# Transposing the normalised input of a fused attention and FFN block by VectorE and DMAs instead of TensorE

## The chip, the cores and the metric

The kernel runs on one core of one Trainium2 chip. The metric is the device time of one execution, in microseconds (us). Engines are named as the profile does: PE is TensorE, DVE is VectorE, ACT is ScalarE, POOL is GpSimd, SP is SyncE, which here does nothing but issue DMAs (its queue appears as SPq).

## The reference

```
x: (16, 512, 256) f32;  8 heads of 128;  FFN 512 -> 1024 -> 1024 -> 256 with weights +1 / -1
xn = (x - mean(x)) / sqrt(var(x) + 1e-5)                 # over the last axis
q, k, v = xn @ wq, xn @ wk, xn @ wv                      # per head
q, k = rope(q), rope(k)
p = softmax(q @ k.T / 128 with a causal mask);  attn = (p @ v) @ wo
h = s0 * [xn, -xn] @ K0;  h = 2 relu(h)                  # K = where(k, 1, -1)
h = s1 * h @ K1;          h = 2 relu(h)
ffn = s2 * h @ K2
out = x + attn + ffn
```

## The kernel before

Work is cut by batch (16 batches of T = 512 tokens) and head (8). One head of one batch is a *slot*; there are 128, and a head's work is spread over three of them. In slot g TensorE, in this order, projects q and k of head g+1 (`project_qk`), forms the four rows of scores of head g (`score_row`), with pieces of the FFN between the rows, adds head g-2's output projection into y (`project_o`), finishes an FFN tile, and multiplies the probabilities of head g-1 with v (`attend(g-1)`). Heads 0 and 1 of a batch have slots of their own form (`slot_of_head_0`, `slot_of_head_1`), because the FFN of the batch before ends there and y is stored.

The order on TensorE is the order of the program, written out by hand. In the first stretch (the start of batch 0) VectorE's order is written out too; on the other engines and queues a scheduler puts each instruction where its inputs are ready by its own model, earlier program text first. `behind(instruction, after)` only ties an instruction's place to one that must be issued before it; in a slot `reduced` is the last row's maximum and `raised` its exponential.

The probabilities must be transposed before `attend`. `turn(g)` (L308) does that without TensorE: VectorE transposes blocks of 32x32 (L314) into a tile z, and 16 DMAs on SP's queue (L321) carry the blocks from each of four groups of 32 partitions to each other group, into pT. z and pT have two buffers each. SP's queue also carries the load of x (L88) and the stores of out (L375).

The normalised input of the next batch is transposed by TensorE: `layernorm` runs in slot 4 of a batch, and in slot 6 `transpose_xn` (L218) makes 8 transposes of 128x128 against an identity (L229) into PSUM. VectorE copies them to xnT (L230), and ScalarE and VectorE split xnT, scaled, into a high and a low half xh, xl (L236, L237), which the first FFN layer `ffn0` (L391) streams in two passes. `project_qk`, in slot 7 for the next batch, and `project_v` read xnT. x of the next batch is loaded in slot 1, into one of two buffers, and the other still holds x for the sum with y.

In x's tile token c*128 + p of the batch lies in partition p, column block c.

Of the kernel before, what the change touches and what calls it, by code (L numbers as in the profile page):

```python
# [9 lines left out]
F32 = mybir.dt.float32  # L10
# [12 lines left out]
def kernel(  # L23
# [60 lines left out]
    ps_y = ctx.enter_context(tc.tile_pool(name="ps_y", bufs=1, space=bass.MemoryType.PSUM))  # L84

    def load_x(b):
        t = xpool.tile([P, NT, M], F32, tag="x", name=f"x_{b}")
        nc.sync.dma_start(t, x[b].rearrange("(c p) m -> p c m", p=P))  # L88
        return t


    xs = {0: xpool.tile([P, NT, M], F32, tag="x", name="x_0")}
    for c in range(NT):
        (nc.scalar if c % 2 else nc.sync).dma_start(xs[0][:, c, :], x[0, ts(c, P), :])
    wv_sb = wpool.tile([P, NM, HD], F32, tag="wv", name="wv_sb")
# [3 lines left out]
    def load_w(engine, sb, w, h0, h1):  # L99
# [8 lines left out]

    k0_sb = [
        hpool.tile([P, 2, F0], U8, tag="h1h", name=f"k0_{c}", bufs=2) for c in range(NM)  # L110
    ]
    k1_sb = work.tile([P, NF0, F1], U8, tag="v", name="k1_sb")
    k2_sb = hpool.tile([P, NF1, M], U8, tag="h1l", name="k2_sb", bufs=2)
    wo_sb = wpool.tile([P, H, M], F32, tag="wo", name="wo_sb")
# [8 lines left out]
    for c in range(NM):  # L123
        nc.sync.dma_start(k0_sb[c], k0.rearrange("(i c p) f -> c p i f", p=P, c=NM)[c])
    load_w(nc.sync, wq_sb, wq, 2, H)
# [35 lines left out]
    def make_w0():  # L161
        for c in range(NM):
            kb = hpool.tile([P, F0], F32, tag="h0h", name=f"kb_{c}")
            nc.vector.tensor_scalar(kb, k0_sb[c][:, 1, :], sg_sb[:, 0:1], None, ALU.mult)
            nc.vector.scalar_tensor_tensor(  # L165
                w0_sb[:, c, :], k0_sb[c][:, 0, :], sg_sb[:, 0:1], kb, ALU.mult, ALU.subtract
            )
# [28 lines left out]

    def layernorm(b, after=None):

        xt = xs[b]
        st = small.tile([P, NT, nc.vector.BN_STATS_DIM], F32, tag="st", name=f"st_{b}", bufs=2)  # L200
        mv = small.tile([P, NT, nc.vector.BN_AGGR_DIM], F32, tag="mv", name=f"mv_{b}", bufs=2)
        for c in range(NT):
            begun = nc.vector.bn_stats(st[:, c, :], xt[:, c, :])
            behind(begun, after)
            nc.vector.bn_aggr(mv[:, c, :], st[:, c, :])
        rs = small.tile([P, NT], F32, tag="rs", name=f"rs_{b}", bufs=2)
        nc.gpsimd.tensor_scalar(rs, mv[:, :, 1], LN_EPS, None, ALU.add)
        raised = nc.gpsimd.tensor_tensor(rs, rs, half_sb, ALU.pow)
        xn = npool.tile([P, NT, M], F32, tag="xn", name=f"xn_{b}")
        for c in range(NT):  # L210
            nc.vector.tensor_scalar(
                xn[:, c, :], xt[:, c, :], mv[:, c, 0:1], rs[:, c : c + 1],
                ALU.subtract, ALU.mult,
            )
        xns[b] = xn
        return raised

    def transpose_xn(b):  # L218
        xn = xns.pop(b)
        xnT = npool.tile([P, NM, T], F32, tag="xnT", name=f"xnT_{b}")  # L220
        xh = npool.tile([P, NM, T], F32R, tag="xh", name=f"xh_{b}")
        xl = npool.tile([P, NM, T], F32R, tag="xl", name=f"xl_{b}")
        xnTs[b], halves[b] = xnT, (xh, xl)
        ready = []
        for m in range(NM):
            pool, tag = (ps_t, "t") if b else (ps_s, "s")
            pt = pool.tile([P, T], F32, tag=tag, name=f"pxn_{b}_{m}")
            for c in range(NT):
                nc.tensor.transpose(pt[:, ts(c, P)], xn[:, c, ts(m, P)], ident)  # L229
            nc.vector.tensor_copy(xnT[:, m, :], pt)  # L230
            if b == 0 and m == NM - 1:
                make_scales()
            ready.append(pt)
            if b or m:
                for n, pt in enumerate(ready, m + 1 - len(ready)):
                    nc.scalar.activation(xh[:, n, :], pt, AF.Identity, scale=c_sb)  # L236
                    nc.vector.scalar_tensor_tensor(  # L237
                        xl[:, n, :], xnT[:, n, :], c_sb, xh[:, n, :].bitcast(F32),
                        ALU.mult, ALU.subtract,
                    )  # L240
                ready.clear()
            yield

    Q = 32
    NQ = P // Q
    NB = NT * (NT + 1) // 2  # L250
    vts, qks, probs, pTs, oTs = {}, {}, {}, {}, {}
# [4 lines left out]
    def project_v(b, g):  # L256
        xnT = xnTs[b]
        vt = work.tile([P, NT, VH * D], F32, tag="v", name=f"v_{b}_{g}")
        vts[b, g] = vt
        for c in range(NT):  # L260
            pv = ps_mm.tile([P, T], F32, tag="mm", name=f"pv_{b}_{g}_{c}")
            for m in range(NM):
                nc.tensor.matmul(  # L263
                    pv, xnT[:, m, ts(c, P)], wv_sb[:, m, ts(g, VH * D)],
                    start=(m == 0), stop=(m == NM - 1),
                )
            nc.scalar.copy(vt[:, c, :], pv)
            yield

    def project_qk(g):  # L270
        b, h = divmod(g, H)
        res = []
        for name, w in (("q", wq_sb), ("k", wk_sb)):
            pq = ps_mm.tile([P, T], F32, tag="mm", name=f"p{name}_{b}_{h}")
            for m in range(NM):
                nc.tensor.matmul(  # L276
                    pq, w[:, m, ts(h, D)], xnTs[b][:, m, :],
                    start=(m == 0), stop=(m == NM - 1),
                )
# [28 lines left out]
    def turn(g, after):  # L308

        zs = work.tile([P, NQ, NB, Q], F32, tag="z", name=f"z_{g}")
# [5 lines left out]
        pT = work.tile([P, NQ, NB, Q], F32, tag="pT", name=f"pT_{g}")  # L318
        for i in range(NQ):
            for j in range(NQ):  # L320
                nc.sync.dma_start(pT[ts(j, Q), i, :, :], zs[ts(i, Q), j, :, :])  # L321
        pTs[g] = pT

    def attend(g):
# [6 lines left out]
        for jc in range(NT):  # L331
            for ic in range(jc, NT):
# [3 lines left out]
                )  # L336
        oT = work.tile([P, T], F32, tag="oT", name=f"oT_{g}")
        nc.vector.tensor_copy(oT, po)
        oTs[g] = oT
# [29 lines left out]
    def store(b):  # L369
        assert y_done[b] == [N_Y] * NT  # L370
        xt = xs.pop(b)
        for i in range(NT // 2):
            rows = xt[:, 2 * i : 2 * i + 2, :]
            nc.vector.tensor_tensor(rows, rows, ys[b][i], ALU.add)
            nc.sync.dma_start(  # L375
                out[b, 2 * i * P : 2 * (i + 1) * P, :].rearrange("(c p) m -> p c m", p=P),
                rows,
            )

# [3 lines left out]
    def ffn0(b, f):  # L383
# [5 lines left out]
        for c in range(NM):  # L389
            for i in range(2):  # L390
                nc.tensor.matmul(  # L391
                    ph, w0_sb[:, c, ts(f, P)], halves[b][i][:, c, :],
                    start=(c == 0 and i == 0), stop=(c == NM - 1 and i == 1),
# [8 lines left out]
    def ffn1(b, f):  # L402
        ph = ps_mm.tile([P, T], F32, tag="mm", name=f"ph1_{b}_{f}")
        for c in range(NF0):
            for i in range(2):
# [4 lines left out]
                if c < NF0 - 1 or i == 0:  # L410
                    yield
        hi = hpool.tile([P, T], F32R, tag="h1h", name=f"h1h_{b}_{f}", bufs=2)
        lo = hpool.tile([P, T], F32R, tag="h1l", name=f"h1l_{b}_{f}", bufs=2)
        nc.scalar.activation(hi, ph, AF.Relu)
# [28 lines left out]
    def first_slot():  # L443
        l0 = [ffn0(0, f) for f in range(NF0)]
        project_qk(1)
        pv = project_v(0, 0)
        next(pv)
        next(pv)
        for ic in range(NT):
            reduced, raised = score_row(0, ic)  # L450
            rest(l0[ic])
            next(pv, None)
        turn(0, reduced)
# [4 lines left out]
    def slot_of_head_0(g):  # L458

        b = g // H  # L460
        if b < B:
            l0 = [ffn0(b, f) for f in range(NF0)]
            project_qk(g + 1)
        else:
            l0 = [iter(())] * NF0
        last = ffn2(b - 1, NF1 - 1)
        for ic in range(NT):
            if b < B:
                reduced, _ = score_row(g, ic)
            if ic == 0:  # L470
# [3 lines left out]
            else:  # L474
                rest(l0[ic - 2])
        if b < B:
            turn(g, reduced)
        project_o(g - 2)
# [6 lines left out]
    def slot_of_head_1(g):  # L485
        b = g // H
        if b < B:
            project_qk(g + 1)
            xs_next(b + 1)
            tile = ffn1(b, 0)  # L490
# [17 lines left out]
    def slot(g):  # L508
# [3 lines left out]
        tile = ffn1(b, h - 1)  # L512
        turned = transpose_xn(b + 1) if h == H - 2 and b + 1 < B else iter(())
        for ic in range(NT):
            reduced, _ = score_row(g, ic)
            if ic == 0:
                rest(ffn2(b, h - 2))
            else:
                some(tile, 4)
            if ic % 2 == 0:  # L520
                next(turned, None)
        turn(g, reduced)
        project_o(g - 2)
        rest(tile)
# [4 lines left out]
        if b + 1 < B:  # L529
            if h == H - 4:  # L530
                layernorm(b + 1, reduced)
            if h == H - 1:
                rest(project_v(b + 1, 0))

    def xs_next(b):
        if b < B:
            xs[b] = load_x(b)

    with tc.manual_schedule(engines={mybir.EngineType.PE}):
        with tc.manual_schedule(engines={mybir.EngineType.DVE}):  # L540
            scale_wq(nc.gpsimd, 0, 2, layernorm(0))
            rest(transpose_xn(0))
            project_qk(0)
            make_w0()
        first_slot()
# [54 lines left out]
```

## Time and profile before

| what | value |
|---|---|
| median of the runs shown | 2207.09 us (2207.02 to 2208.16, 3 runs) |
| profiled execution, its own time | 2207.65 us |
| its span, first to last instruction | 2205.8 us |
| instructions on PE (matmul) | 9856, busy 2182.0 us (99%) |
| VectorE, ScalarE, GpSimd busy | 1195.6 us (54%), 868.7 us (39%), 950.5 us (43%) |
| transposes of xn on PE | 128, mean 283 ns each |
| DMAs pT<-z on SP's queue | 2048, 40 KB each, 1.9 us from issue to landing |

The profile is of one execution. A line of it names the source line, the engine, the operation and its tiles (output <- inputs), then how often it ran, the busy time in us and the mean of one in ns. Matmuls overlap, so the duration of one is longer than the pitch at which they follow each other; the pitch is read from the chain, which follows the work that ended last back to the start. For a queue such as SPq, a duration is the time that its sequencer takes to issue the DMA; the landing comes later.

### The profile page before, as it was taken

To read this page: it belongs to the slowest core of one execution; us is meant where nothing else is said; L and a number is where in the kernel's file an instruction comes from. 1 tells how busy PE (TensorE), PEld (TensorE's weight loads), DVE (VectorE), ACT (ScalarE), POOL (GpSimd) and SP (SyncE) were. 2 spreads that over 40 slices of the span, in tenths; PEclk is the share of its full clock that TensorE was granted. 3 is DMA by queue.
4 is the path that set the end of the run, shared out by engine and by line. 5 is a ranking of instruction groups with operands and counts; after the bars stand their busy time and mean duration, and the time that the engine had idled before them with its cause. 6 is when DMAs were issued, how large, how long until landed. Compare 5 with 4: busy or idle time off the path is not lost.

```text
span 2205.8 us, 30324 instructions
## 1 busy us (share of the span) xinstructions
PE 2182.0 (99%) x9856; PEld 1561.9 (71%) x9856; DVE 1195.6 (54%) x2993; ACT 868.7 (39%) x1959; POOL 950.5 (43%) x1067
## 2 busy tenths in 40 slices
PE   7999999999999999999999999999999999999998
PEld 4677777777777777776777777777667777777766
DVE  6555655556555565554655555555555645556544
ACT  4334333344434344344343433443333443433432
POOL 4443534435343353434534354353443534435342
PEclk9999999999999999999999999999999999999999
DMA  4112111121111211112111121111211111121111
GB/s 150 42 43 56 43 51 46 38 56 48 51 42 37 57 46 56 40 39 57 46 53 43 38 57 46 53 41 36 56 48 55 37 46 48 46 56 40 43 43 51
DMA packets 121676, 109.28 MB, mean 50 GB/s; under 512 B 35248, under 2 KB 120240, under 8 KB 121520
## 3 DMA queue, kind: packets, MB, share of 16 engines
q1 hardware_dynamic: 120384, 106.57, 18.0%
q8 instruction: 79, 1.29, 0.3%
q10 hardware_dynamic: 1136, 0.79, 0.1%
q14 instruction: 77, 0.63, 0.1%
HBM read 14.94 MB, written 8.39 MB: 11 GB/s over the span
## 4 chain that ended last, share of the span: by engine, by line
PE 97%; SPq 1%; DVE 1%; ACT 1%; issue 0%; POOL 0%; DMA 0%; POOLq 0%; ACTq 0%
PE ph L406 21%; PE y L356 15%; PE po L333 13%; PE s L295 12%; PE pv L263 10%; PE pq L276 10%; PE pk L276 10%; PE ph L391 5%; SPq L321 1%; PE pxn L229 1%; DMA pT<-z 0%; DMA x<-in_L_attn_x_dram 0%; DVE z L314 0%; DVE w_sb L165 0%; DVE h0l L399 0%
## 5 line engine op out<-in xcount | busy, mean ns | idle before, releaser
L286 POOL TENSOR_TENSOR swq<-swq,sin_sb 128x512 f32<-128x512 f32 x128 | 165.5, 1293 | 969.3 <-ACT swq L283 969.3
L406 PE MATMUL ph<-h0h,w_sb 128*128 128x512 f32 x1024 | 517.5, 505 | 0.0
L301 ACT ACTIVATE p<-s,nmax 128x128 f32<-128x128 f32 (+3 forms) x512 | 270.6, 529 | 361.1 <-DVE nmax L298 326.5
L406 PE MATMUL ph<-h0l,w_sb 128*128 128x512 f32 x1024 | 408.7, 399 | 0.0
L295 PE MATMUL s<-kT,qT 128*128 128x128 f32 (+3 forms) x1024 | 360.7, 434 | 1.9 <-ACT p L301 1.9
L304 POOL TENSOR_SCALAR p<-p,rl 128x128 f32<-128x128 f32 (+3 forms) x512 | 269.4, 537 | 200.7 <-DVE rl L303 199.1
L285 DVE TENSOR_TENSOR qT<-pq,cos_sb 128x512 f32<-128x512 f32 x128 | 88.6, 692 | 461.7 <-ACT swq L283 461.6
L333 PEld LDWEIGHTS po<-pT,v 128*128 128x128 f32 x2560 | 306.2, 192 | 19.9 <-PE ph L406 6.1
L333 PE MATMUL po<-pT,v 128*128 128x128 f32 x2560 | 308.4, 276 | 5.8 <-DMA pT<-z 4.4
L314 DVE STREAM_TRANSPOSE z<-p 128x128 f32<-128x128 f32 (+3 forms) x512 | 234.2, 490 | 68.2 <-POOL p L304 67.5
L298 DVE TENSOR_REDUCE nmax<-s 128x1 f32<-128x128 f32 (+3 forms) x512 | 251.5, 491 | 13.2
L295 PEld LDWEIGHTS s<-kT,qT 128*128 128x128 f32 x1024 | 182.7, 189 | 89.0 <-issue 62.0
L406 PEld LDWEIGHTS ph<-h0h,w_sb 128*128 128x128 f32 x1024 | 193.0, 188 | 73.2 <-issue 26.9
L406 PEld LDWEIGHTS ph<-h0l,w_sb 128*128 128x128 f32 x1024 | 193.2, 189 | 72.7 <-issue 26.8
L276 PE MATMUL pq<-xnT,wq_sb 128*128 128x512 f32 x512 | 242.6, 596 | 0.0
L356 PE MATMUL y<-wo_sb,oT 128*128 128x256 f32 x1024 | 241.8, 379 | 0.0
L276 PE MATMUL pk<-xnT,wk_sb 128*128 128x512 f32 x512 | 240.6, 592 | 0.0
L263 PE MATMUL pv<-wv_sb,xnT 128*128 128x512 f32 x512 | 227.2, 596 | 0.0
L356 PEld LDWEIGHTS y<-wo_sb,oT 128*128 128x128 f32 x1024 | 192.6, 189 | 29.7
L282 ACT COPY swq<-pq 64x512 f32<-64x512 f32 x128 | 74.6, 583 | 329.0 <-PE pq L276 327.4
L276 PEld LDWEIGHTS pk<-xnT,wk_sb 128*128 128x128 f32 x512 | 97.4, 190 | 123.0 <-issue 122.5
L296 DVE TENSOR_TENSOR s<-s,causal 128x128 f32<-128x128 f32 x512 | 150.3, 294 | 56.5 <-PE s L295 56.5
(61 smaller groups left out, 2519.9 us busy)
## 6 DMA issues: line engine op xcount, KB each, us to landing
pT<-z SPq DMA_DIRECT2D x2048, 40.0 KB, 1.9
out_dram<-x SPq DMA_DIRECT2D x32, 256.0 KB, 2.2
x<-in_L_attn_x_dram SPq DMA_DIRECT2D x15, 512.0 KB, 3.9
wv_sb<-in_L_attn_wv_dram SPq DMA_DIRECT2D x2, 512.0 KB, 9.3
k_sb<-in_L_ffn_k_dram SPq DMA_DIRECT2D x1, 1024.0 KB, 10.8
wo_sb<-in_L_attn_wo_dram SPq DMA_DIRECT2D x1, 1024.0 KB, 10.7
wq_sb<-in_L_attn_wq_dram SPq DMA_DIRECT2D x1, 768.0 KB, 6.8
wk_sb<-in_L_attn_wk_dram SPq DMA_DIRECT2D x1, 768.0 KB, 8.4
```

The source lines that it names most:

```text
L263: nc.tensor.matmul(pv, xnT[:, m, ts(c, P)], wv_sb[:, m, ts(g, VH * D)], start=(m == 0), stop=(m == NM - 1),)
L276: nc.tensor.matmul(pq, w[:, m, ts(h, D)], xnTs[b][:, m, :], start=(m == 0), stop=(m == NM - 1),)
L286: nc.gpsimd.tensor_tensor(sw, sw, sin_sb, ALU.mult)
L295: nc.tensor.matmul(ps[:, :n], qT[:, ts(ic, P)], kT[:, :n], start=True, stop=True)
L296: nc.vector.tensor_tensor(ps[:, ts(ic, P)], ps[:, ts(ic, P)], causal, ALU.add)
L298: reduced = nc.vector.tensor_reduce(nmax, ps[:, :n], AX.X, ALU.max, negate=True)
L301: raised = nc.scalar.activation(p, ps[:, :n], AF.Exp, bias=nmax, accum_out=l)
L304: nc.gpsimd.tensor_scalar(p, p, rl, 1.0, ALU.mult, ALU.mult)
L314: behind(nc.vector.transpose(zs[:, :, block(ic, 0) : block(ic + 1, 0), :].rearrange("p j c a -> p c j a"), p.rearrange("p (c j a) -> p c j ...
L333: nc.tensor.matmul(po[:, ts(ic, P)], vt[:, jc, ts(h % VH, D)], pT[:, :, block(ic, jc), :], start=(jc == 0 and ic == 0), stop=(jc == ic), s ...
L356: nc.tensor.matmul(ys[b][c // 2][:, c % 2, :], lhsT[:, ts(c, P)], rhs, start=(y_done[b][c] == 0 and c % 2 == 0), stop=(y_done[b][c] == N_Y ...
L406: nc.tensor.matmul(ph, w1_sb[:, c, ts(f, P)], h0s[b][i][:, c, :], start=(c == 0 and i == 0), stop=(c == NF0 - 1 and i == 1),)
```

## The change

xn of the next batch goes the way of the probabilities: four VectorE transposes and 16 DMAs, in slot 4 after `turn`, with z's tag and buffers for the blocks on their way (`transpose_xn`, `carry`). For this the rows of x are dealt differently: token i*128 + c*32 + a lies in partition i*32 + a, column block c, so that tokens come out of the block transposes in their natural order in xnT. Loads and stores of x become four DMAs each, of 32 partitions. Where the rows of the sum must stand as in x's tile, the order (c i a) is put in by access patterns: the FFN's first layer streams `tokens_by_row`, and the copy of attend's output oT is permuted.

The rest follows from it. The load of x is at the end of slot 2 instead of the head of slot 1, the layernorm in slot 3 instead of 4, and the split into halves one instruction each on ScalarE and VectorE, tied to slot 7. xnT has two buffers; oT, h1h and h1l have one. The first batch keeps TensorE's transposes, from a separate load of x, while the x for its sum is loaded once more in the new order; one half of w0's making moves from VectorE to ScalarE, and the v projection stands as one piece at the head of the first slot. In the last slot of head 0, attend comes after all of the FFN.

```diff
     def load_x(b):
         t = xpool.tile([P, NT, M], F32, tag="x", name=f"x_{b}")
-        nc.sync.dma_start(t, x[b].rearrange("(c p) m -> p c m", p=P))
+        for i in range(NQ):
+            nc.sync.dma_start(t[ts(i, Q)], rows_of(x, b, i))
         return t
...
+    xs[0] = load_x(0)
     load_w(nc.sync, wq_sb, wq, 2, H)
...
-            nc.vector.tensor_scalar(kb, k0_sb[c][:, 1, :], sg_sb[:, 0:1], None, ALU.mult)
+            nc.scalar.activation(kb, k0_sb[:, c, 1, :], AF.Identity, scale=sg_sb[:, 0:1])
...
+    def carry(to, blocks):
+
+        for i in range(NQ):
+            for j in range(NQ):
+                nc.sync.dma_start(to[ts(j, Q), i], blocks[ts(i, Q), j])
...
+    def tokens(t, m):
+        return t[:, :, m].rearrange("p i c a -> p i (c a)")
+
+    def tokens_by_row(t, m):
+        return t[:, :, m].rearrange("p i c a -> p c i a")
+
+    def transpose_xn(b, after):
         xn = xns.pop(b)
+        zx = work.tile([P, NQ, NM, NT, Q], F32, tag="z", name=f"zx_{b}")
+        for c in range(NT):
+            behind(nc.vector.transpose(
+                zx[:, :, :, c, :].rearrange("p j m a -> p m j a"),
+                xn[:, c, :].rearrange("p (m j a) -> p m j a", j=NQ, a=Q),
+            ), after)
+        new_xnT(b)
+        carry(xnTs[b], zx)
...
+    def split_xn(b, reduced=None, raised=None):
+
+        xh = npool.tile([P, NQ, NM, NT, Q], F32R, tag="xh", name=f"xh_{b}")
+        xl = npool.tile([P, NQ, NM, NT, Q], F32R, tag="xl", name=f"xl_{b}")
+        halves[b] = xh, xl
+        flat = "p i m c a -> p (i m c a)"
+        behind(nc.scalar.activation(
+            xh.rearrange(flat), xnTs[b].rearrange(flat), AF.Identity, scale=c_sb
+        ), raised)
+        behind(nc.vector.scalar_tensor_tensor(
+            xl.rearrange(flat), xnTs[b].rearrange(flat), c_sb,
+            xh.rearrange(flat).bitcast(F32), ALU.mult, ALU.subtract,
+        ), reduced)
...
-                    ph, w0_sb[:, c, ts(f, P)], halves[b][i][:, c, :],
+                    ph, w0_sb[:, c, ts(f, P)], tokens_by_row(halves[b][i], c),
...
-            nc.sync.dma_start(
-                out[b, 2 * i * P : 2 * (i + 1) * P, :].rearrange("(c p) m -> p c m", p=P),
-                rows,
-            )
+        for i in range(NQ):
+            nc.sync.dma_start(rows_of(out, b, i), xt[ts(i, Q)])
...
+        if b == B:
+            rest(ffn1(b - 1, NF1 - 1))
+            project_o(g - 2)
+            rest(ffn2(b - 1, NF1 - 2), last)
+            attend(g - 1)
+            return
...
-        turned = transpose_xn(b + 1) if h == H - 2 and b + 1 < B else iter(())
         for ic in range(NT):
-            reduced, _ = score_row(g, ic)
+            reduced, raised = score_row(g, ic)
             if ic == 0:
                 rest(ffn2(b, h - 2))
             else:
                 some(tile, 4)
-            if ic % 2 == 0:
-                next(turned, None)
         turn(g, reduced)
+        if h == H - 4 and b + 1 < B:
+            transpose_xn(b + 1, reduced)
         project_o(g - 2)
...
-            if h == H - 4:
-                layernorm(b + 1, reduced)
+            if h == H - 5:
+                layernorm(b + 1, xs[b + 1], reduced)
+            if h == 2:
+                xs[b + 1] = load_x(b + 1)
             if h == H - 1:
+                split_xn(b + 1, reduced, raised)
                 rest(project_v(b + 1, 0))
```

## The prediction

> **What bounds the kernel now.** I read the page first (busy shares, chain), then the chain between 236 and 290 us, then the SyncE queue's timeline, then the TensorE clock by windows.
>
> ```profile
> span 2205.8 us, 30324 instructions
> PE 2182.0 (99%) x9856; PEld 1561.9 (71%) x9856; DVE 1195.6 (54%) x2993; ACT 868.7 (39%) x1959; POOL 950.5 (43%) x1067
> ...
> PE 97%; SPq 1%; DVE 1%; ACT 1%; issue 0%; POOL 0%; DMA 0%; POOLq 0%; ACTq 0%
> ```
>
> TensorE is never free: 97% of the chain is its own instructions. So a TensorE instruction taken out is worth its place in the chain, and any wait put before one costs in full. What a transpose is worth stands in the chain (start, us, what; po is attend; the pieces are attend(4), (5) and (6) of batch 1, the number being the head, and the transposes lie in slot 6):
>
> ```profile
> 254.25 2.23 PE po L333 x20
> ...
> 261.08 0.44 PE pxn L229 x4
> ...
> 264.45 0.44 PE pxn L229 x4
> ...
> 269.31 2.23 PE po L333 x20
> ...
> 283.52 2.23 PE po L333 x20
> ```
>
> From attend to attend the slot with transposes takes 15.06 us, the next one 14.21. Eight transposes are worth 0.86 us.
>
> The second resource is the queue of SyncE (SPq), which issues DMAs in order. Here are the 16 DMAs pT<-z of turn(4) of batch 1, of turn(5), and the row of all:
>
> ```profile
> 240.21 10.01 SPq L321 DMA_DIRECT2D pT<-z  x16
> ```
> ```profile
> 254.40 10.01 SPq L321 DMA_DIRECT2D pT<-z  x16
> ```
> ```profile
> L321 SPq DMA_DIRECT2D pT<-z x2048: 507/589/1906, 41.0 to 2193.2; - x187
> ...
> DMA to landing us min/median/max: 1.8/1.9/4.0
> ```
>
> Issuing 16 takes 10.01 us (0.63 us each) of a slot of 14.2: the queue is idle for 254.40 - 250.22 = 4.18 us. The 16 of 254.40 end at 264.41; the last lands 1.3 us later, at 265.7 (1.9 us from its issue). The attend that reads them starts at 269.15 in the trace: 3.4 us to spare, the transposes' 0.86 among them. At attend(1) of a batch it is only about 0.7 us. TensorE's two longest waits on the way (engine, line, what for; us, times, longest):
>
> ```profile
> PE po L333 <- DMA pT<-z: 4.4, 3, 2.5
> PE ph L391 <- DVE w_sb L165: 2.4, 1, 2.4
> ```
>
> Three attends ever wait for pT, one attend(1) and the last two of the kernel. A later turn has to use up its slack first, and is then paid in full.
>
> Last, the clock (columns: stretch, length, PE, PEld, DVE, ACT, POOL, granted clock, DMA share, GB/s). A stretch of 3.4 us in which TensorE was idle for about 2.4 is followed by 3.4 us at half clock:
>
> ```profile
> 23.90:27.30 3.40, 0.99 (x5) 0.56 (x4) 3.17 (x4) 0.05 (x1) 3.37 (x2) 1.00 0.63 178
> 27.30:30.70 3.40, 3.40 (x6) 1.32 (x5) 0.76 (x2) 0.95 (x3) 2.09 (x3) 0.50 0.00 0
> ```
>
> **The change, part by part.**
>
> *Transposes off TensorE*, in 15 of 16 batches: -0.86 us each, -12.9 in all. Here the Trainium skill ("TensorE: Matmul & The Clock Gate", Part 4: PE-mode transpose) prices one at about 275 ns in a kernel, and the trace's row has 283 ns for the mean instruction. By that, eight are worth 2.2 us and 15 batches 33 us. But these instructions overlap; their pitch in the chain is 0.44 / 4 = 0.11 us. I take the pitch.
>
> *In their place, VectorE*: four transposes of 128x256 in slot 4, by the row of the same form (z<-p 128x256) 407 ns, 1.6 us; out of slot 6 go two copies (0.68) and two splits (0.75), 2.9 us. VectorE is at 54% and fills pauses: the layernorm's BN instructions in the trace go in while z waits for GpSimd. So zx is ready by about 241.7, turn(4) is not delayed, cost 0. Were that cover gone, h1l behind it would come 1.6 us later, with about 4 us before TensorE reads it.
>
> *16 more DMAs on SPq* (carry of zx, 32 partitions to 32 partitions, rows of 1 KB where pT's have 1280 B). They stand in program order behind the 16 of turn(4) and ahead of those of turn(5). The nearest row is pT's, 0.63 us a piece; the cheapest DMAs of the trace (x loads and stores, 0.38 us an instruction, 0.42 with the gap) are the lower end, 6.7 us for 16; the upper end is 11.3 us, the slowest turns. I take pT's price, same partitions and form: 10.0, and 10.2 as the mean of all 128 turns. Then, on the clock of batch 1: turn(4) ends at 250.2, carry 260.3, turn(5), ready since 254.3, starts 6 us late and ends at 270.4, landing at 271.7. TensorE reaches attend(5) at 269.15 - 0.86 = 268.3, and waits 3.4 us. With the actual ends of turn(4) in the 15 batches, read off the queue's timeline, and 10.24 for the rest, the mean wait is 4.2 us (3.8 to 5.1). A rule speaks against this: the skill ("DMA: Bandwidth & Descriptors", Issuing engines are not separate DMA queues) calls the sequencer's time to start a DMA usually small beside the DMA. By it the wait is nil and the sum is the first rival's. Here 16 issues cost 10 us and a landing 1.9; the trace decides. What is queued behind is only turn(5): turn(6) has its z at 268.8 and SPq free at 270.4, still 2 us or more ahead of its attend once that has moved too. So one wait per batch. zx also takes one of two z buffers: turn(5)'s first transposes need turn(4) landed at 251.5, and begin at 251.64; a miss of up to 1.3 us falls inside the queue's delay. Cost 0.
>
> *The clock after that wait.* An idle of 4.2 us mostly covers 2.4 of one 3.4 us stretch, and the half-clock stretch after it costs up to 1.7 us. Some of it falls into the wait itself, sometimes the idle is split: +1.1 us (0 to 1.7).
>
> *Loads and stores of x*: four DMAs instead of one or two. At 183 to 193 us SPq has nothing between turn(0) and turn(1) but 1.17 us of stores and one load of 0.38, so even at 0.63 us all eight fit into the 9.5 us; after turn(2) there are 10 us free. 0, at worst +0.3 us a batch from attend(1)'s thin margin. Below nothing: that margin is lost to slow issues of turn(1) itself, which starts when z is ready, so an earlier queue gains nothing.
>
> *Permuted operands.* ffn0 now streams runs of 32, as attend does (2.23 / 20 = 0.112 us for 128 columns, against 6.87 / 64 = 0.107 for the contiguous pv). 0; at worst 4 x 4.4 ns x 512 = 9 us. A broken-up read has no way to be faster. The oT copy (0.69) lies a slot ahead of its reader.
>
> *The split in slot 7*: ScalarE one instruction of 1024 columns, 1.1 to 1.25 us (rows 128x768, 832 ns; 128x1024, 1236), VectorE about 1.4. attend(7) comes after pv and half a slot, with 12 to 13 us to spare. 0. Single buffers of oT, h1h, h1l: on TensorE the last reader stands before the next writer's source. 0.
>
> *Start.* kb on ScalarE takes 2.3 us off VectorE's way to w0, and all of pv stands before the first ffn0: up to the 2.4 and 0.7 us that TensorE waits at 23 to 27 us, and the half clock after (1.7). Against it: ScalarE gets 2.5 us more ahead of v copies, pv may wait for a PSUM buffer, and 512 KB more go ahead of wq's rest. -5 to +4; I take -2.
>
> *End.* ffn2's last piece (1.0 us) moves ahead of the last attend into an idle of 2.5 us, so the half clock there may go too; against it the oT copy is exposed and three stores start after both additions. 0 (-2 to +2).
>
> Sum: 15 x (4.2 - 0.86 + 1.1) = +66.6; -2. The profiled execution took 2207.65 us (span 2205.8), 0.56 above the median shown: 2272.3, less 0.56, is 2272.
>
> **The rivals.**
> 1. *Faster: the queue's delay never reaches TensorE.* Point of decision: 16 carries must issue in 4.2 (idle) + 2.5 (slack) = 6.7 us, 0.42 each, exactly the price of the x DMAs; or the scheduler puts them where the queue is free (10 us before turn(3)). For it: 512-row DMAs at 0.38. Against: not one turn is under 10.0. Then -12.9 - 2: 2192. Chance 0.17.
> 2. *A cheaper carry*, 0.50 to 0.57 us an issue: wait 2 to 3 us, the clock rarely halved, +1.3 to +2.5 a batch: 2225 to 2245. Chance 0.13. At 0.43 to 0.47 wait and gain cancel: no change, 0.05.
> 3. *Carry ahead of turn(4).* If the zx transposes all get ahead of z's last, turn(4) is late by 10 us and attend(4) by 7.6: +8.4 a batch with the clock, 2330. Two of four fit into the pause of 0.8 us, so 0.04.
> The main case has 0.61, its own range 2245 to 2295.
>
> **How the numbers follow.** 0.2% is about what this measurement can tell from no change: 4.4 us. Faster 0.17, same 0.05, slower 0.78. The range goes from 2200 (just inside no change) to 2300.
>
> **What would show it.** In the profile after: no pxn outside the start; some 2288 SBUF-to-SBUF DMAs on SPq; "PE po <- DMA pT<-z" with 15 or more waits of 3 to 5 us, in slot 6 of each batch alone; SPq busy without pause from turn(4) through turn(5); half-clock stretches behind these waits. It is wrong if carry's issues take under 0.45 us, if they stand elsewhere in the queue, or if slots other than 6 grow: ffn0's matmuls over 233 ns would mean the permuted reads.

## The result: 4% slower, and the profile after

| | before | after |
|---|---|---|
| median of the runs (5 of each) | 2207.09 us | 2299.65 us (2296.59 to 2300.91) |
| ratio | 1 | 1.0416, 95% interval 1.0401 to 1.0432 |
| profiled execution, its span | 2207.65, 2205.8 us | 2296.59, 2294.6 us |
| granted TensorE clock, mean share of full speed | 0.998 | 0.982 |

The page of the changed kernel, where the share of TensorE in the chain is read first:

```profile
span 2294.6 us, 30678 instructions
PE 2205.4 (96%) x9736; PEld 1576.8 (69%) x9736; DVE 1191.7 (52%) x3005; ACT 867.1 (38%) x1945; POOL 943.7 (41%) x1067
...
PE 86%; SPq 8%; DMA 2%; issue 1%; DVE 1%; ACT 1%; POOL 0%; POOLq 0%; DVEq 0%; ACTq 0%
```

TensorE has 120 instructions fewer and is busy longer, which already points at the clock. Its part of the chain fell from 97% to 86%; 8% went to SyncE's queue and 2% to DMAs. No other engine did more work. The queue's timeline of batch 1, in two windows (start, duration, what; x32 is turn(5) and turn(6)):

```profile
244.56 10.01 SPq L235 DMA_DIRECT2D pT<-z  x16
```
```profile
254.67 10.04 SPq L235 DMA_DIRECT2D xnT<-zx  x16
264.82 20.91 SPq L235 DMA_DIRECT2D pT<-z  x32
```

The queue does not stop from turn(4) through turn(6). The 16 carries took 10.04 us, and turn(5), whose z was ready at 258.9, begins at 264.82. TensorE at that place, before the change and after it, and the row of all the waits ("who waited for it" at L235, where turns and carries are both issued):

```profile
269.15 2.39 PE L333 MATMUL po<-pT,v 128*128 128x128 f32 x20
```
```profile
272.35 0.39 PE L434 MATMUL ph<-h0l,w_sb 128*128 128x512 f32 x1
276.54 4.10 PE L360 MATMUL po<-pT,v 128*128 128x128 f32 x20 [3.80 <-issue]
```
```profile
L235 SPq DMA_DIRECT2D pT<-z x2048: 507/589/1742, 40.4 to 2281.9; - x187
L235 SPq DMA_DIRECT2D xnT<-zx x240: 507/589/1375, 114.0 to 2111.2; - x120
...
  PE po L360: 68.1, 19
```

Attend(5) waits 3.80 us. The profile names "issue" here, and in other batches the DMA pT<-z; but in all 15 batches attend(5) starts 0.41 or 0.44 us after the last DMA of turn(5) has landed (here at 276.13), so the landing is what it waited for. Of the 19 waits, the 15 in slot 6 make 65.6 us, 3.8 to 5.0 each. Once it starts, attend takes 4.10 us where it took 2.39. The windows by stretches of the clock show why (stretch, length, PE, PEld, DVE, ACT, POOL, granted clock, DMA share, GB/s); the first two rows are batch 1, the others batch 2:

```profile
273.40:276.80 3.40, 0.26 (x2) 0.29 (x3) 0.69 (x1) 0.04 (x1) 0.00 (x0) 1.00 0.24 63
276.80:280.20 3.40, 3.40 (x18) 3.40 (x18) 0.00 (x0) 0.00 (x0) 0.00 (x0) 0.50 0.23 60
413.40:416.80 3.40, 0.41 (x2) 0.00 (x0) 1.19 (x2) 0.60 (x1) 0.00 (x0) 0.99 0.25 64
416.80:420.20 3.40, 1.81 (x8) 1.84 (x9) 0.00 (x0) 0.00 (x0) 0.00 (x0) 0.50 0.29 72
420.20:423.60 3.40, 3.40 (x15) 2.92 (x14) 0.57 (x1) 0.00 (x0) 0.00 (x0) 0.50 0.17 42
423.60:427.00 3.40, 3.40 (x12) 1.71 (x11) 0.74 (x2) 1.26 (x3) 0.56 (x1) 1.00 0.27 70
```

In batch 1 one stretch runs at half clock. In batch 2 the wait reaches 1.6 us into the half-clock stretch, TensorE is busy for only 1.81 us of it, and the next, wholly busy stretch is at half clock too. A second half-clock stretch came in 8 of the 15 batches.

Slots from attend to attend, means of 14 batches: the slot to attend(5) went from 15.07 to 18.76 us and the slot to attend(6) from 14.20 to 16.48. An undisturbed slot is 14.20, so the two hold 6.84 us too much, 4.4 of it the wait. Of the remaining 2.4, the slot to attend(6) holds 2.3: that is the half clock. The rest is the end of the last matmul before the wait (0.39 us long at a pitch of 0.23), which otherwise overlaps with the next one.

### The profile page after: what moved, and what is told of

It reads as the page before. It is cut to its first block, busy times and chain, and to the rows that moved or that the text cites. A ratio compares the mean times of both kernels' runs of the same rounds, so it can differ in the third digit from the quotient of the medians.

```text
span 2294.6 us, 30678 instructions
## 1 busy us (share of the span) xinstructions
PE 2205.4 (96%) x9736; PEld 1576.8 (69%) x9736; DVE 1191.7 (52%) x3005; ACT 867.1 (38%) x1945; POOL 943.7 (41%) x1067
## 4 chain that ended last, share of the span: by engine, by line
PE 86%; SPq 8%; DMA 2%; issue 1%; DVE 1%; ACT 1%; POOL 0%; POOLq 0%; DVEq 0%; ACTq 0%
PE ph L434 17%; PE po L360 13%; PE y L386 13%; PE s L326 10%; PE pv L294 10%; PE pq L307 9%; PE pk L307 9%; SPq L235 8%; PE ph L419 5%; DMA pT<-z 1%; DVE z L343 0%; DMA x_first<-in_L_attn_x_dram 0%; ACT swq L314 0%; ACT swq L313 0%; DVE qT L316 0%
## 5 line engine op out<-in xcount | busy, mean ns | idle before, releaser
L360 PE MATMUL po<-pT,v 128*128 128x128 f32 x2560 | 335.8, 291 | 68.6 <-DMA pT<-z 39.2
L360 PEld LDWEIGHTS po<-pT,v 128*128 128x128 f32 x2560 | 330.3, 206 | 87.0 <-issue 73.6
L307 PE MATMUL pq<-xnT,wq_sb 128*128 128x512 f32 x512 | 247.8, 607 | 0.0
L366 DVE COPY oT<-po 128x512 f32<-128x512 f32 x128 | 88.4, 690 | 182.0 <-PE po L360 182.0
```

What stands on the lines that cost most here:

```text
L307: nc.tensor.matmul(pq, w[:, m, ts(h, D)], tokens(xnTs[b], m), start=(m == 0), stop=(m == NM - 1),)
L360: nc.tensor.matmul(po[:, ts(ic, P)], vt[:, jc, ts(h % VH, D)], pT[:, :, block(ic, jc), :], start=(jc == 0 and ic == 0), stop=(jc == ic), s ...
```

## The experiments

The theory was that 16 more issues ahead of turn(5) on SyncE's queue make pT late, and that wait and clock are all of the loss. The rivals were the rest of the change (layout, loads and stores in four pieces, permuted reads) and a cost of the transfers themselves, by contention or longer landings.

**The carry alone, in the kernel before.**

```diff
+        if h == H - 5 and b + 1 < B:
+            layernorm(b + 1, reduced)
+        if h == H - 4 and b + 1 < B:
+            zx = work.tile([P, NQ, NM, NT, Q], F32, tag="z", name=f"zx_{b}")
...
+            dd = npool.tile([P, NQ, 144], F32, tag="dd", name=f"dd_{b}")
+            for i in range(NQ):
+                for j in range(NQ):
+                    nc.sync.dma_start(dd[ts(j, Q), i], blocks[ts(i, Q), j, 0:144])
```

> The kernel before, unchanged in layout and with its TensorE transposes, plus the suspected part alone: layernorm one slot earlier, and in slot 4 four VectorE transposes and 16 DMAs of 32 partitions into a scratch tile that nothing reads (rows of 576 B, for want of room; one buffer of oT instead of two). Queue theory: turn(5) is late as in the changed kernel, but TensorE reaches attend(5) 0.86 us later, so the wait is about 3.5 us, with 1.5 to 2.5 us of half clock: 15 x 5 to 6 us, 2280 to 2297 us. Layout rival: 2207 us.

Measured: 2293.20 us, ratio 1.0394 (1.0380 to 1.0409). The queue's timeline of batch 1 (the last row is turn(5) and part of turn(6)), and TensorE's waits for pT, the last two of the kernel among them:

```profile
256.82 10.03 SPq L539 DMA_DIRECT2D dd<-zx  x16
266.96 18.40 SPq L321 DMA_DIRECT2D pT<-z  x28
```
```profile
PE po L333 <- DMA pT<-z: 52.9, 16, 4.2
PE po L333 <- issue: 3.1, 1, 3.1
```

Rows of 576 B cost as much as rows of 1024: 10.03 us for 16. The waits in slot 6 are 52.5 us in all, 3.5 a batch, and half clock follows each of them. So this one part, with nothing reading its result, brings 86 us. (The earlier layernorm and the single oT buffer, which came in with it, cost nothing of that size: the next run has both.)

**The rest of the change, without the carry.**

```diff
-        if h == H - 4 and b + 1 < B:
-            transpose_xn(b + 1, reduced)
+        turned = transpose_by_pe(b + 1) if h == H - 2 and b + 1 < B else iter(())
```

(`transpose_by_pe` makes the 8 transposes as before and copies them into the new xnT in permuted order.)

> The changed kernel with all of its new layout, loads, stores, buffers and permuted reads, but the transposes of every batch back on TensorE in slot 6, copied in the permuted order; no carry and no VectorE transposes. Queue theory: no late turn, no wait; before's time plus the permuted reads, 2207 + 2 - 1 = 2207 to 2210 us. Layout rival: most of the loss stays, 2280 us or more.

Measured: 2209.60 us, ratio 1.0012 (1.0005 to 1.0020). TensorE's waits for pT, none of them in slot 6:

```profile
PE po L372 <- DMA pT<-z: 2.4, 4, 0.8
```

The slots to attend(0) and attend(7) are 18.13 and 24.86 us here as in the changed kernel, against 18.04 and 24.80 before: 0.14 us a batch, 2.2 of the 2.5 us in all. The layout rival is out.

**The carry where the queue is free.**

```diff
-        if h == H - 4 and b + 1 < B:
-            transpose_xn(b + 1, reduced)
...
-            if h == H - 5:
+            if h == 2:
                 layernorm(b + 1, xs[b + 1], reduced)
-            if h == 2:
-                xs[b + 1] = load_x(b + 1)
+                transpose_xn(b + 1, reduced)
```

(The load goes to slot 1, after the store.)

> The changed kernel with the carry moved to where SyncE's queue is free: x loaded in slot 1, layernorm and the VectorE transposes in slot 2, so that the 16 carries stand between turn(2) and turn(3), where the queue is idle for about 10 us. Queue theory: the carries (10.0 us) just fit, turn(3) is late by 0 to 1 us against 2.5 us of slack; about 2196 us, some us more where slow issues exceed the slack. Rival (the carries cost wherever they stand, by contention or longer landings): waits of some us at attend(3) instead of attend(5), 2250 us or more. Rival (layout): 2290 to 2300 us.

Measured: 2195.83 us, ratio 0.9952 (0.9940 to 0.9965). The same 16 DMAs, one after the other between turn(2) and turn(3):

```profile
206.69 10.80 SPq L235 DMA_DIRECT2D pT<-z  x16
217.59 10.04 SPq L235 DMA_DIRECT2D xnT<-zx  x16
227.73 10.03 SPq L235 DMA_DIRECT2D pT<-z  x16
```

They take as long, no attend(3) waits, and an undisturbed batch takes 135.01 us (135.75 before). The contention rival is out as well: what costs is the place in the queue.

**Work put into the wait.**

```diff
         rest(tile)
+        if h == H - 2 and b + 1 < B:
+            rest(project_v(b + 1, 0))
         attend(g - 1)
...
                 split_xn(b + 1, reduced, raised)
-                rest(project_v(b + 1, 0))
```

> The changed kernel with one thing moved: the v projection of the next batch (6.9 us of TensorE work that needs only xnT) from the end of slot 7 to slot 6, ahead of attend(5). Queue theory (16 carries ahead of turn(5) on SyncE's queue make pT late, TensorE waits 4.4 us there and then runs at half clock): the late turn is covered by 6.9 us of work, no wait on pT in slot 6 and no half-clock stretch in mid-kernel; 2207 - 12.9 (transposes gone) + 2.1 (permuted reads) - 0.5 to 1 (start) = about 2196 us. Rival (the new layout, the four-piece loads and stores or the permuted reads cost the time): the move changes nothing, 2290 to 2300 us.

Measured: 2195.84 us, ratio 0.9945 (0.9932 to 0.9959). The carry still stands ahead of turn(5). The chain of batch 1:

```profile
255.56 2.23 PE po L360 x20
269.74 6.87 PE pv L294 x16
276.60 2.23 PE po L360 x20
290.81 2.23 PE po L360 x20
```

pv fills the place of the wait, and the next slot is 14.2 us again: without the wait there was no half clock in mid-kernel.

**The clock by itself.** Matmuls whose result nothing reads, ahead of attend(5):

```diff
+        if h == H - 2 and b + 1 < B:
+            pd = ps_t.tile([P, T], F32, tag="t", name=f"pd_{g}")
+            for n in range(10):
+                nc.tensor.matmul(
+                    pd, wq_sb[:, 0, 0:D], tokens(xnTs[b], 0), start=(n == 0), stop=(n == 9),
+                )
         attend(g - 1)
```

> The changed kernel with ten matmuls of 128x512 (4.3 us) put ahead of attend(5) in slot 6, whose result nothing reads; TensorE is busy while pT is late. What it tells apart: the wait of 4.4 us stays in another form, and if the half clock after it is the rest of the loss (15 x 2.4 = 36 us), it goes: 2299.7 - 36 = 2263 us. Rival (the slots after the wait are longer for another reason, a late turn(6) or a full ScalarE): nothing changes, 2296 to 2305 us.

Measured: 2329.12 us, ratio 1.0554 (1.0538 to 1.0571), a miss. Each of these f32 matmuls of 512 columns appears as two instructions, 0.43 us apart, so ten take 8.6 us, twice what was meant. The half clock did go (mean clock 0.998, slot to attend(6) 14.28 us). With five:

> As the run with the filled wait, with five matmuls instead of ten. An f32 matmul of 128x512 runs as two passes of 0.43 us, so the ten took 8.6 us, twice the wait; five take 4.3 us, just the wait. If the half clock is the rest of the loss, its 2.4 us a batch go and nothing else changes: 2299.7 - 36 = 2263 us, slots to attend(6) back at 14.2 to 14.3 us. Rival: 2300 us.

Measured: 2269.16 us, ratio 1.0278 (1.0260 to 1.0295). The mean granted clock is 0.998 again (0.982 in the changed kernel). TensorE now works through 4.3 us that it had waited, and the kernel is 30 us faster than the changed one. The slot to attend(6) is 14.26 us. The 6 us to the forecast are mostly what is left of the wait, in the nine batches where turn(5) was late by more than the filler (5.6 us in all).

**Part of the carry on ScalarE's queue.**

```diff
-                nc.sync.dma_start(to[ts(j, Q), i], blocks[ts(i, Q), j])
+                on = nc.scalar if act and i == NQ - 1 else nc.sync
+                on.dma_start(to[ts(j, Q), i], blocks[ts(i, Q), j])
```

> The changed kernel with 4 of the 16 carries (those from the last 32 partitions) issued on ScalarE's queue, where a pause follows; slot, data and order otherwise the same. Queue theory: SyncE's queue has 12 carries, 7.5 us, turn(5) comes 2.5 us earlier, the wait at attend(5) falls from 4.4 to 1.9 us. On the clock: if it takes about 2.4 us of idle in a stretch, half clock goes altogether: 2196 + 15 x 1.9 = 2224 us. If idle of 1.6 us is enough (as in the second stretches of the changed kernel), up to 15 x 1.7 more, 2250 us. Rival (longer landings or contention of the transfers themselves): unchanged, 2300 us.

Measured: 2246.40 us, ratio 1.0183 (1.0169 to 1.0197). The waits are 32.5 us in slot 6, 2.2 a batch (4.4 with 16 carries on SyncE), and 9 of 15 are still followed by a half-clock stretch; in batch 1 a wait of 1.82 us within one stretch was enough:

```profile
267.00:270.80 3.80, 1.98 (x13) 1.47 (x12) 1.40 (x2) 0.60 (x1) 0.51 (x1) 0.99 0.25 65
270.80:274.20 3.40, 3.40 (x16) 3.20 (x15) 0.29 (x1) 0.00 (x0) 0.00 (x0) 0.50 0.22 56
```

With 8 of 16 (`i >= NQ // 2`):

> As the run with four, with 8 of the 16 carries on ScalarE's queue. Queue theory: 8 carries, 5.0 us, end within the pause of 4.2 us and the slack of 2.5: no wait, no half clock, 2196 us, and ScalarE's 5 us of issues may hold the next q and k copies up by 2 us, which have a slot to spare: up to 2200. Rival (contention): 2300 us.

Measured: 2224.53 us, ratio 1.0081 (1.0068 to 1.0095). No wait on pT is left in slot 6, as forecast, but the time is a miss by 28 us. ScalarE's timeline and TensorE's waits:

```profile
242.75 5.31 ACTq L236 DMA_DIRECT2D xnT<-zx  x8
248.18 0.58 ACT L314 COPY swq<-pq 64x512 f32<-64x512 f32 x1 [5.55 <-DMA xnT<-zx]
```
```profile
PE s L327 <- ACT p L333: 23.6, 16, 2.5
```

The eight issues hold ScalarE for 5.3 us, the copies of q and k and with them the exponentials of slot 5 come late, and TensorE waits for a scores buffer (23.6 us in all, 1.9 of them at the start); two of these waits are followed by a half-clock stretch, which costs 3.4 us together. The slot to attend(4) went from 14.20 to 16.16 us. An issue of this kind costs its engine 0.6 to 0.7 us, on SyncE and on ScalarE.

**The permuted reads.** On top of pv in slot 6, the split writes the halves in the order of x's rows:

```diff
-        xh = npool.tile([P, NQ, NM, NT, Q], F32R, tag="xh", name=f"xh_{b}")
+        xh = npool.tile([P, NM, NT, NQ, Q], F32R, tag="xh", name=f"xh_{b}")
...
-                    ph, w0_sb[:, c, ts(f, P)], tokens_by_row(halves[b][i], c),
+                    ph, w0_sb[:, c, ts(f, P)], halves[b][i][:, c].rearrange("p c i a -> p (c i a)"),
```

> The kernel with the v projection in slot 6, and the high and low halves written in the order of x's rows by the split (two instructions on ScalarE, eight on VectorE), so that ffn0 streams contiguous columns again. If the permuted reads are what makes slots 0 and 7 longer by 0.14 us a batch: 16 x 0.14 = 2.2 us less, 2193.6 us and the slots to attend(0) and attend(7) back by 0.08 and 0.06 us. Rival (the extra comes from the split or the four-piece loads): no change, 2196 us.

Measured: 2193.67 us, ratio 0.9942 (0.9930 to 0.9955). Against the run with pv alone the intervals overlap, so the medians do not decide; the slots do. The slot to attend(0) is back at 18.04 us (18.13), that to attend(7) at 17.94 (17.99), and an undisturbed batch takes 134.86 us instead of 135.01. By its slots this is the fastest version here, 0.6% under the kernel before; pv alone and the carry in slot 2 are 0.5% under it.

## Why the prediction was right in kind and 28 us short

Forecast 2272 (2200 to 2300), measured 2299.65: the direction and the mechanism held. The size did not: the time lies 0.35 us inside the range's upper end, which is luck, and above the main case's own range (2245 to 2295). Step by step, on the profiled executions (88.9 us apart where 64.6 were forecast; the medians are 92.6 apart):

- *Transposes off TensorE*, -0.86 a batch: right. With the wait covered, an undisturbed batch fell from 135.75 to 135.01 us; that is -0.86 and the permuted reads' +0.14. The pitch, not the instruction's duration, was the price.
- *Carry at pT's price behind turn(4)*, 10.0 us: right; 10.02 to 10.80, mean 10.29. Its rows are shorter, and that made no difference. (The slowest turn before took 11.6 us, a little over the 11.3 of the forecast.)
- *Wait at attend(5)*: forecast 4.2, measured 4.4, the 15 waits between 3.8 and 5.0. Right, also that no other slot's attend waits for a turn made late. In the sum for batch 1, 3.4 us against 3.8, the 0.41 us from the landing to attend's start are missing.
- *The clock after the wait*: this term was mis-sized. Forecast 1.1 us a batch (0 to 1.7), measured 2.3, which is 18 of the 24 us missing. The forecast had one half-clock stretch behind a wait, and for some waits none. In the trace half clock follows each of the 15 waits: each left TensorE idle for 2.42 us or more of one full-clock stretch, so even the 2.4 us that the forecast asked for would have caught them all. Half of TensorE's busy time in these stretches is 1.4 us a batch. The larger part of the miss is the second half-clock stretch, which the forecast put at nothing: it came in 8 batches, where the wait reached 0.7 us or more into the first, and cost 13.7 us, 0.9 a batch. The run with five matmuls agrees: 30 us faster, with 5.6 us of waits left.
- *Permuted operands*: taken as 0, bound 9 us. Measured 0.14 us a batch, 2.2 in all; the contiguous variant takes it away again.
- *Loads and stores of x, the split, the single buffers*: 0, right; attend(1) waited 1.0 us in all against 2.2 before. (Before, seven attends waited 0.1 us or more for pT and not three: five attends(1) and the last two, each starting within 0.5 us of the landing. The profile puts four of them down to a matmul.)
- *Start*, -2: attend(0) came 0.5 us earlier in the changed kernel, and in the experiments with the same start between 0.4 earlier and 2.7 later; no gain can be claimed. The trace has TensorE waiting for the v copies there instead of for w0. *End*: 0, right; from the last attend to the end 10.67 and 10.69 us.

Of the rivals, "the queue's delay never reaches TensorE" did not come true as the kernel stands, but its own condition, a place where the queue is free, was tried and gives 2196 us where the forecast said 2192. A cheaper carry and a carry ahead of turn(4) were seen nowhere.

## What to carry to other kernels

A step taken off the bounding engine is paid for on another resource, and that one is to be priced where it is put: here 16 DMA issues of 0.63 us stood in a queue with a pause of 4.2 us and 2.5 us of slack, while ten microseconds were free two slots earlier. Look for the queue's pauses first, and for work that can stand in front of the late reader. A wait of TensorE can cost more than its length: a wait of 4.4 us took another 2.3 us in half clock here.

## What the runs showed of the hardware that was not expected

- The granted clock kept to stretches of 3.41 us: in mid-kernel the changed kernel was at half clock for 3.41 or 6.83 us at a time, and at full clock for 136.53 us, 40 stretches, between. I laid the waits of slot 6 over these stretches, in the changed kernel, in the carry alone and in the run with four carries on ScalarE, 45 waits. Idle of 1.82 us or more within a stretch at full clock was followed by half clock every time, 1.71 us or less never; a wait of 2.6 us that fell as 0.95 and 1.64 us on two stretches cost no clock.
- Elsewhere in the traces that limit did not hold: near the start of the kernel before, a stretch with 1.91 us of idle (47.78 to 51.20 us) was followed by full clock, and near the end of the run with four carries on ScalarE 1.52 us (2230.01 to 2233.43) were enough for half clock. What else counts stays open.
- In the same three runs, a stretch at half clock in slot 6 was followed by another when TensorE idled for 0.70 us or more of it (15 waits did so much), and by full clock at 0.61 us or less.
- Issuing a DMA between groups of 32 partitions took 0.63 us for rows of 576, 1024 and 1280 B alike on SyncE, and 5.31 / 8 = 0.66 us on ScalarE (batch 1; 0.63 to 0.85 in the 15 batches).
- Streaming ffn0's columns in runs of 32 cost 0.14 us over 32 matmuls of 512 columns, 4.5 ns each, in each batch.
